# Nyström attention layer: scores in other PSUM banks, a variance one slot later, one block of attention in another place

## The chip, the cores and the metric

The kernel runs on one core of one Trainium2 chip. The time is device microseconds of one execution, the median of three. A profile is one execution of its own, with its own time.

## What is computed

The input x is (2, 512, 64, 32): two batches of 512 channels by 2048 tokens, all in fp32. Layer 0 is softmax attention with eight heads of 64 channels, frequency and time embeddings appended to the channels of its queries and keys, and a residual. Layer 1 normalises its input, and applies Nyström attention with 256 landmarks, a residual convolution of 33 tokens over the values, an output projection with bias, and a residual. A feed-forward map with a norm follows, again with a residual. Cut to layer 1 and the map, the computation is:

```
q, k, v = split(norm(x1) @ Wqkv)                      # 8 heads of 64, 2048 tokens
ql, kl  = mean of q, k over groups of 8 tokens         # 256 landmarks
attn1 = softmax(q kl^T / 8); attn2 = softmax(ql kl^T / 8); attn3 = softmax(ql k^T / 8)
z = pinv(attn2)                                        # 6 iterations of
    # z = 0.25 z (13 I - xz (15 I - xz (7 I - xz))),  xz = attn2 z
o = attn1 @ (z @ (attn3 @ v)) + conv33(v)
x2 = x1 + o @ Wout + bout
out = x2 + (normalised x2) @ map
```

## The kernel before, in words

**Engines and their order.** TensorE, VectorE, ScalarE and GpSimd take their instructions in the order in which the program writes them; no planner moves them. The DMAs are issued from SP's queue. So the order of the program's calls is the order of each queue, and an instruction that waits holds up all behind it on its engine.

**Tiles.** A block is 512 tokens (`TB`), so a batch has four blocks (`NTB`); channels lie in four chunks of 128 (`KC`). Heads go in pairs, four pairs (`NPAIR`) to a batch, eight in all. The kernel divides PSUM into eight banks of 128 x 512 fp32. In the stage that makes keys, queries and `attend` for batch 0's pairs, two of them are a ring `pp` that `bank(...)` hands out in turn, four are two double banks `sc` (`scores_bank`), two serve the values. In the later stage `pp` has four banks, a ring `pr` for the inverse's products has two (`product_bank`), and two side banks serve attn3's and attn1's values.

**Batch 0's pairs.** `attend` (L1243) makes attn2 of a pair: four products into `sc2` (L1254), exp (L1261), row sums and scaling on VectorE. It lies among the products of keys and queries (L1214), and among layer 0's last norm: its mean (L961) and variance (L974) with the sums of VectorE (L957, L958; squares L970, L971).

**The loop over pairs.** The main loop goes over `todo`: the four pairs of batch 1, then those of batch 0, n = 0 to 7. In turn n the pair in hand has its pseudo-inverse: five iterations of two squares, of `M` into `pa` and of `R` into `pb` (L1506), with VectorE updating `R` and `M` behind each (L1519). After each iteration `chunk(c)` puts in work of other pairs: block c of attn1 of the pair before (scores L1563, exp L1568, sum L1572, values L1579, row sums L1587, reciprocals L1595, ends L1600 and L1601) and the scores, exponentials, sums and values of attn3 of the pair after (L1335, L1344, L1349, L1356). Chunk 4 has landmarks and the convolution instead. Then come three products of another form (L1481), each with a flip (`tp`, L1490), and `last(0)` to `last(5)` stand between them; values of a later pair (L924) and other things are put in there.

**Finishing a block.** After turn 4 a generator `finish1_units` writes batch 1's outputs, block by block, in units that `advance(finish)` takes one at a time in the turns n = 5, 6 and 7, from `chunk`, from `last` and from a string of letters behind the loop. A block's units are: four output products `yp` with the residual added on VectorE (L939, L946); the sums and the mean (L957, L958, L961), the subtraction (L962), the squares on ScalarE and VectorE (L965 to L971), the variance (L974) and its root (L976), the reciprocal (L1625); and four products `fp` of the map (L1654) with y (L1646), the residual (L1647) and the store (L1648). A unit `GAP` takes one call without work. The residual `xb` is loaded (L1612) into a buffer that the next block uses too, tag `xr`, so that a load waits for the stores of the block before.

**The end.** Behind turn 7 a string gives the order of the last pair's attn1 (`1`), the finish units (`f`), batch 0's output products (`a`, `b`) and their norms (`s`, `t`). Then a loop over t does `map_units` for batch 0's four blocks, with the next block's norm between.

Of the kernel before, what the change touches and what calls it, by code (L numbers as in the profile page):

```python
# [16 lines left out]
P = 128  # L17
B, C, H, W = 2, 512, 64, 32
S = H * W
KC = C // P  # L20
# [641 lines left out]
def fast_path(  # L662
# [62 lines left out]
    def chunked(ap):  # L725
        return ap.rearrange("(k p) n -> p k n", p=P)

    def bank(name):
        return ps.tile([P, 512], F32, tag="pp", name=name)

    def scores_bank(name):
        return ps.tile([P, 2, 512], F32, tag="sc", name=name)
# [21 lines left out]
    def row_of(name):  # L754
        return apool.tile([P, TB], F32, tag="rinv", name=name)
# [37 lines left out]
    def gap(n=1):  # L793
        for _ in range(n):
            yield GAP
# [387 lines left out]
    class Pair:  # L1183
# [59 lines left out]
        def attend(self):  # L1243

            i, L = self.i, self.L
            X = self.X = [zpool.tile([P, 2, LM + 1], F32, tag=f"M{h}", name=f"X_{i}_{h}") for h in range(2)]
            rs = small.tile([P, 4], F32, tag="rs2", name=f"rs2_{i}")
            for h in range(2):
                nc.gpsimd.memset(X[h][:, :, LM:], 1.0)
            for h in range(2):  # L1250
                rows_h = slice(h * D, (h + 1) * D)
                sc = bank(f"sc2_{i}_{h}")
                for t in range(2):
                    nc.tensor.matmul(  # L1254
                        sc[:, t * LM : (t + 1) * LM],
                        lhsT=L[0][rows_h, t * P : (t + 1) * P],
                        rhs=L[1][rows_h, :],
                        start=True,
                        stop=True,
                    )  # L1260
                nc.scalar.activation(X[h][:, :, :LM], sc.rearrange("p (t n) -> p t n", n=LM), AF.Exp)  # L1261
            for h in range(2):
                two = slice(2 * h, 2 * h + 2)
                x_h = X[h][:, :, :LM]
                nc.vector.tensor_reduce(rs[:, two], x_h, AX.X, ALU.add)
                nc.vector.reciprocal(rs[:, two], rs[:, two])
                nc.vector.tensor_tensor(
                    x_h, x_h, rs[:, two].unsqueeze(2).to_broadcast([P, 2, LM]), ALU.mult
                )
                nc.sync.dma_start(X_d[self.b, self.hp, h], x_h)  # L1270
                nc.vector.tensor_reduce(rsum[:, i, two], x_h, AX.X, ALU.add)
# [54 lines left out]
            self.av3 = side_bank(3, f"av3_{self.name}")  # L1326
            self.p3 = {}

        def attn3_scores(self, s):
            scs = [bank(f"sc3_{self.name}_{s}_{h}") for h in range(2)]  # L1330
            for j in range(2):
                for h in range(2):
                    rows = slice(h * D, (h + 1) * D)
                    c = 2 * s + j
                    nc.tensor.matmul(  # L1335
                        scs[h][:, j * LM : (j + 1) * LM],
                        lhsT=self.k[rows, c * P : (c + 1) * P],
                        rhs=self.L[0][rows, :],
                        start=True,
                        stop=True,  # L1340
                    )
            p = self.p3[s] = exps(f"p3_{self.name}_{s}")
            for h in range(2):
                nc.scalar.activation(p[:, h, :], scs[h], AF.Exp)  # L1344
# [258 lines left out]
    class Finish1:  # L1603
# [25 lines left out]
        def norm_units(self):  # L1629
            steps = self.steps(lambda: deviation(self.name))  # L1630
            next(steps)
            yield GAP
            next(steps)
            yield
            next(steps)
            yield GAP
            next(steps)
            yield

        def map_units(self, bank_of):  # L1640


            def rest(m, fp):
                xb, toks = self.xb, slice(self.t * TB, (self.t + 1) * TB)
                y = row_of(f"y_{self.name}_{m}")
                nc.vector.tensor_tensor(y, fp, self.rstd, ALU.mult)  # L1646
                nc.vector.tensor_tensor(xb[:, m, :], y, xb[:, m, :], ALU.add)  # L1647
                nc.sync.dma_start(chunked(out[self.b])[:, m, toks], xb[:, m, :])  # L1648

            last = None  # L1650
            for m in range(KC):
                fp = bank_of(m, f"fp_{self.name}_{m}")
                for k in range(KC):
                    nc.tensor.matmul(  # L1654
                        fp, lhsT=mT[:, k, m * P : (m + 1) * P], rhs=self.xn[:, k, :],
                        start=k == 0, stop=k == KC - 1,
                    )
                if last is not None:
                    rest(*last)
                last = m, fp  # L1660
                yield
            rest(*last)

# [204 lines left out]
    for n, pair in enumerate(todo):  # L1868
        before = todo[n - 1] if n else None
        after = todo[n + 1] if n + 1 < len(todo) else None  # L1870
        if n + 2 < len(todo):
            todo[n + 2].prefetch_w()
        if n == NPAIR + 2:
            before.load_o(kvpool.tile([P, S], F32, tag="k", name=f"o2_{n - 1}"))
        if n == NPAIR + 3:
            before.load_o(late_buffer(f"o2_{n - 1}"))
        pair.iteration_start()
        while vals:
            advance(vals)
        if after:  # L1880
            after.prefetch()
            after.attn3_begin()
        if n + 2 < len(todo):
            vals = [values(n + 2)]
        if n:
            q = late_buffer if n > NPAIR + 1 else lambda name: kvpool.tile([P, S], F32, tag="k", name=name)
            pair.prefetch1(q(f"q2_{pair.name}"))

        def chunk(c):
            nonlocal landmarks  # L1890
            if before and c:
                before.attn1_inverse(c - 1, 1)
                before.attn1_end(c - 1)
            advance(finish)
            if c == NTB:
                if after:
                    landmarks = after.landmarks_values()
                    next(landmarks)
                    drain(convolution(n + 1))
                else:  # L1900
                    advance(finish, 2)
                return
            if before:
                if c:
                    before.attn1_scores(c, 0)
                    before.attn1_scores(c, 1)
                before.attn1_add(c)
            if after:
                for s in (2 * c, 2 * c + 1):
                    after.attn3_scores(s)  # L1910
                    after.attn3_add(s)
            else:
                advance(finish)
            if before:
                before.attn1_values(c)
            if after:
                after.attn3_values(2 * c)
            else:
                advance(finish)
            if before:  # L1920
                before.attn1_sums(c)
            if after:
                after.attn3_values(2 * c + 1)
            if before:
                before.attn1_inverse(c, 0)
            if n == NPAIR + 2 and c % 2:
                advance(finish)

        def last(i):
            nonlocal start  # L1930
            if i == 1 and after:
                next(landmarks)
                drain(landmarks)
                start = after.start_values()
            if i == 2 and after:
                next(start)
            else:
                advance(vals)
            if i == 3 and after:
                next(start)  # L1940
            if i == 5:
                pair.attn1_scores(0, 0)
                pair.attn1_scores(0, 1)
            advance(finish)

        landmarks = start = None
        pair.pinv(chunk, last)
        if n == NPAIR:
            finish.append(finish1_units(1, [p.o for p in todo[:NPAIR]]))
# [43 lines left out]
    st = [f.steps(deviation_of(t)) for t, f in enumerate(fs)]  # L1993

    ones_last = last_attn1()
    for c in "1f1f1f1f1f1fa1a1a1a1s1bs1s1b1bbt":
        if c == "f":
            advance(finish)
        else:
            next({"1": ones_last, "a": outs[0], "b": outs[1], "s": st[0], "t": st[1]}[c])  # L2000
# [13 lines left out]
    nc.gpsimd.partition_all_reduce(bad, oks, P, bass_isa.ReduceOp.max)  # L2014

    for t in range(NTB):
        maps = fs[t].map_units(wide_banks)
        if t + 1 < NTB:
            if t:
                next(st[t + 1])  # L2020
            turns(maps, None, st[t + 1], None, st[t + 1], None, None, st[t + 1])
        else:
            drain(maps)
        if t + 2 < NTB:
            drain(outs[t + 2])
# [89 lines left out]
```

## Time and profile before

| what | us |
|---|---|
| median of three runs | 2808.86 (2808.78 to 2810.7) |
| the profiled execution | 2808.29 |
| its span, first to last instruction | 2806.2 |
| TensorE busy | 2745.0 (98%) |
| VectorE busy | 1778.3 (63%) |
| ScalarE busy | 913.5 (33%) |
| GpSimd busy | 231.7 (8%) |

The mean granted clock of TensorE was 0.993. A line of the timeline has the start and the duration in microseconds, the engine, the line of the program, the operation, the tile written and the tiles read, the shape, the number of instructions run together, and in brackets the idle time before with the engine, tile and line that ended it. A line of waits has who waited, for whom, the microseconds in total, how often, and the longest. Products in fp32 appear as two rows each, so that eight products count as sixteen.

### The profile page before, as it was taken

What the parts mean: (1) busy time and instruction counts of PE and PEld (TensorE: products, weight loads), DVE (VectorE), ACT (ScalarE), POOL (GpSimd) and SP (SyncE); (2) the same over time, 40 slices, a digit from 0 to 9 for tenths busy, and PEclk for the clock granted to TensorE, in tenths of its full rate; (3) what the DMA queues carried; (4) which work ended last, traced back from release to release, by engine and by line L of the source; (5) the groups of instructions that cost most, each with busy time, mean ns of one, the idle gap of its engine ahead of it and who ended that gap; (6) DMA issues with size and microseconds to landing.
All of it is one profiled execution on the core that took longest, in us unless ns stands there. A gap on an engine that the chain in (4) does not pass through costs nothing. (4 is left out here: it accounts for less than half of the span.)

```text
span 2806.2 us, 39647 instructions
## 1 busy us (share of the span) xinstructions
PE 2745.0 (98%) x16746; PEld 1374.3 (49%) x16746; DVE 1778.3 (63%) x2109; ACT 913.5 (33%) x1352; POOL 231.7 (8%) x130
## 2 busy tenths in 40 slices
PE   9999999999999999999999999999999999999899
PEld 5343443434343334343344455777667666554333
DVE  2868788784658775767767544545755655556565
ACT  1434343433334334434422223223332323222110
POOL 1101101010101210100002000000100100000000
PEclk9999999999999999999999999999999999999999
DMA  3000000101001200002025632203001102010201
GB/s 113 5 5 1 5 1 1 61 16 46 27 32 60 75 1 1 1 31 67 16 83 180 202 120 89 97 28 114 27 28 50 65 1 86 23 61 19 101 16 46
DMA packets 85626, 140.31 MB, mean 50 GB/s; under 512 B 7856, under 2 KB 42944, under 8 KB 82880
## 3 DMA queue, kind: packets, MB, share of 16 engines
q1 hardware_dynamic: 80944, 120.87, 12.8%
q0 software_dynamic: 4416, 16.79, 1.6%
q8 instruction: 133, 2.18, 0.3%
q14 instruction: 53, 0.43, 0.0%
q10 hardware_dynamic: 80, 0.03, 0.0%
HBM read 82.48 MB, written 55.19 MB: 49 GB/s over the span
## 5 line engine op out<-in xcount | busy, mean ns | idle before, releaser
L1058 DVE TENSOR_TENSOR acc_f<-acc_f,p_f 128x1024 f32<-128x1024 f32 x448 | 611.4, 1365 | 217.8 <-ACT p_f L1048 188.8
L1048 ACT ACTIVATE p_f<-sc_f 128x1024 f32<-128x1024 f32 x512 | 496.8, 1022 | 580.2 <-PE sc_f L1040 574.1
L1040 PE MATMUL sc_f<-q_f,k_f 64*64 64x512 f32 x4096 | 491.7, 595 | 2.9 <-ACT p_f L1048 2.9
L1070 PE MATMUL av_f<-p_f,v_f 64*64 64x512 f32 x4096 | 484.3, 589 | 0.0
L1070 PEld LDWEIGHTS av_f<-p_f,v_f 64*64 64x64 f32 x4096 | 156.5, 133 | 283.0 <-issue 283.0
L1040 PEld LDWEIGHTS sc_f<-q_f,k_f 64*64 64x64 f32 x4096 | 144.8, 133 | 293.8 <-issue 253.0
L1214 PE MATMUL pp<-xh,w 128*128 128x512 f32 x512 | 231.2, 604 | 4.6 <-ACT X L1261 3.9
L1214 PEld LDWEIGHTS pp<-xh,w 128*128 128x128 f32 x512 | 95.7, 192 | 125.8 <-issue 113.9
L1506 PE MATMUL pb<-R 128*128 128x192 f32 (+1 forms) x640 | 149.6, 380 | 1.0 <-DVE M L1519 1.0
L1506 PE MATMUL pa<-M 128*128 128x192 f32 (+1 forms) x640 | 150.6, 380 | 0.0
L1595 DVE RECIPROCAL acc<-acc 128x256 f32<-128x256 f32 x64 | 111.4, 1746 | 46.7 <-ACT acc L1590 46.7
L1089 POOL TENSOR_TENSOR q_f<-q_f,rinv_f 128x512 f32<-128x512 f32 x32 | 68.3, 2135 | 825.6 <-DVE rinv_f L1088 825.5
L1601 POOL TENSOR_TENSOR o<-o,acc 128x512 f32<-128x512 f32 x32 | 53.8, 1682 | 885.1 <-DVE acc L1600 778.1
L924 PE MATMUL vp<-w,xh 128*128 128x128 f32 x1024 | 122.3, 278 | 0.0
L924 PEld LDWEIGHTS vp<-w,xh 128*128 128x128 f32 x1024 | 118.6, 194 | 7.2 <-issue 4.2
L924 PEld LDWEIGHTS vp_f<-wv_f,x 128*128 128x128 f32 x1024 | 115.6, 192 | 12.7 <-issue 11.0
L879 PE MATMUL pp_q_f<-x,wq_f 128*128 128x512 f32 x256 | 117.5, 612 | 4.2 <-DVE q_f L882 3.1
L939 PE MATMUL yp_f<-q_f,wo_f 128*128 128x512 f32 x256 | 115.9, 606 | 4.2 <-DVE rinv_f L1088 3.3
L924 PE MATMUL vp_f<-wv_f,x 128*128 128x128 f32 x1024 | 118.5, 276 | 0.0
L1506 PEld LDWEIGHTS pb<-R 128*128 128x128 f32 x640 | 106.5, 190 | 24.4 <-DVE M L1519 2.1
L1506 PEld LDWEIGHTS pa<-M 128*128 128x128 f32 x640 | 108.2, 193 | 20.4 <-ACT M L1497 2.5
L1654 PE MATMUL fp_g<-xn_g,mT 128*128 128x512 f32 x256 | 115.1, 598 | 0.7 <-ACT p L1568 0.7
(202 smaller groups left out, 3009.6 us busy)
## 6 DMA issues: line engine op xcount, KB each, us to landing
xh<-xh_fd SPq DMA_DIRECT2D x12, 1024.0 KB, 5.4
xr_f<-in_x_dram SPq DMA_DIRECT2D x8, 1024.0 KB, 5.1
x_fd<-xr_f POOLq DMA_DIRECT2D x8, 1024.0 KB, 4.7
xh_fd<-xn_f POOLq DMA_DIRECT2D x8, 1024.0 KB, 4.6
k_fd<-k SPq DMA_DIRECT2D x32, 256.0 KB, 2.7
q_fd<-q SPq DMA_DIRECT2D x32, 256.0 KB, 3.0
xb_g<-x_fd SPq DMA_DIRECT2D x32, 256.0 KB, 4.5
k<-k_fd SPq DMA_DIRECT2D x8, 1024.0 KB, 5.9
```

What stands on the lines that cost most here:

```text
L879: nc.tensor.matmul(pp, lhsT=w_sb[kind][:, k, cols], rhs=xbs[t][:, k, :], start=k == 0, stop=k == KC - 1)
L924: nc.tensor.matmul(vp[:, j * P : (j + 1) * P], lhsT=xb[:, k, j * P : (j + 1) * P], rhs=w_of(k), start=k == 0, stop=k == KC - 1,)
L939: nc.tensor.matmul(yp, lhsT=wo_sb[:, k, m * P : (m + 1) * P], rhs=oTs[k][:, toks], start=k == 0, stop=k == NPAIR - 1,)
L1040: nc.tensor.matmul(sc[r * D : (r + 1) * D, h, :], lhsT=hd.k[rows, lo : lo + D], rhs=hd.q[rows, t * TB : (t + 1) * TB], start=True, stop=True,)
L1048: nc.scalar.activation(p, sc, AF.Exp, scale=D**-0.5)
L1058: nc.vector.tensor_tensor(acc, first if c == 1 else acc, p, ALU.add)
L1070: nc.tensor.matmul(av[r][half, :], lhsT=hd.v[keys, c, half], rhs=pp[keys, h, :], start=c == 0, stop=c == NST - 1,)
L1089: nc.gpsimd.tensor_tensor(o, o, rinv, ALU.mult)
L1214: nc.tensor.matmul(pp, lhsT=self.w[j][:, c, :], rhs=xhs[t][:, c, :], start=c == 0, stop=c == KC - 1)
L1506: nc.tensor.matmul(dst, lhsT=lhsT[:, k, t * P : (t + 1) * P], rhs=rhs[:, k, :], start=k == 0, stop=k == 1)
L1595: nc.vector.reciprocal(half, half)
L1654: nc.tensor.matmul(fp, lhsT=mT[:, k, m * P : (m + 1) * P], rhs=self.xn[:, k, :], start=k == 0, stop=k == KC - 1,)
```

## The change

It has five parts. For pairs 0 to 2 of batch 0 `attend` takes both heads' scores from one double bank `sc` in place of two banks of `pp`. In each chunk the first of attn3's two score blocks takes the two product banks `pr` in place of two of `pp`. In the finishing units the variance comes two free calls behind its squares in place of one, and so each later unit of batch 1 moves by one call for each block done. In turns 6 and 7 the fourth block of attn1 of the pair before is taken out of chunk 3, and stands in `last(0)` to `last(5)`. The very last product of the map is made in two halves of 256 columns, each with its own y, residual and store. The string of the last turns is changed to hold the two more units that are left over.

```diff
         def attend(self):
+            scs = scores_bank(f"sc2_{i}") if i + 1 < NPAIR else None
...
-                sc = bank(f"sc2_{i}_{h}")
+                sc = scs[:, h, :] if scs is not None else bank(f"sc2_{i}_{h}")
...
-        def attn3_scores(self, s):
-            scs = [bank(f"sc3_{self.name}_{s}_{h}") for h in range(2)]
+        def attn3_scores(self, s, bank_of=bank):
+            scs = [bank_of(f"sc3_{self.name}_{s}_{h}") for h in range(2)]
...
         def norm_units(self):
...
             next(steps)
-            yield GAP
+            yield from gap(2)
             next(steps)
             yield
...
-        def map_units(self, bank_of):
+        def map_units(self, bank_of, parts=1):
-            def rest(m, fp):
-                xb, toks = self.xb, slice(self.t * TB, (self.t + 1) * TB)
-                y = row_of(f"y_{self.name}_{m}")
-                nc.vector.tensor_tensor(y, fp, self.rstd, ALU.mult)
-                nc.vector.tensor_tensor(xb[:, m, :], y, xb[:, m, :], ALU.add)
-                nc.sync.dma_start(chunked(out[self.b])[:, m, toks], xb[:, m, :])
+            def rest(m, fp, cols):
+                xb, toks = self.xb, slice(self.t * TB + cols.start, self.t * TB + cols.stop)
+                y = row_of(f"y_{self.name}_{m}_{cols.start}")[:, cols]
+                nc.vector.tensor_tensor(y, fp[:, cols], self.rstd[:, cols], ALU.mult)
+                nc.vector.tensor_tensor(xb[:, m, cols], y, xb[:, m, cols], ALU.add)
+                nc.sync.dma_start(chunked(out[self.b])[:, m, toks], xb[:, m, cols])
...
+                n = TB // (parts if m == KC - 1 else 1)
+                for lo in range(0, TB, n):
+                    cols = slice(lo, lo + n)
+                    for k in range(KC):
+                        nc.tensor.matmul(
+                            fp[:, cols], lhsT=mT[:, k, m * P : (m + 1) * P], rhs=self.xn[:, k, cols],
+                            start=k == 0, stop=k == KC - 1,
+                        )
+                    if last is not None:
+                        rest(*last)
+                    last = m, fp, cols
...
         def chunk(c):
-            if before and c:
+            if before and 0 < c <= n_ones:
                 before.attn1_inverse(c - 1, 1)
                 before.attn1_end(c - 1)
...
-            if before:
+            ones_before = before if c < n_ones else None
+            if ones_before:
...
-                for s in (2 * c, 2 * c + 1):
-                    after.attn3_scores(s)
+                for s, bank_of in ((2 * c, product_bank), (2 * c + 1, bank)):
+                    after.attn3_scores(s, bank_of)
                     after.attn3_add(s)
...
         def last(i):
+            if n_ones < NTB:
+                if i == 0:
+                    before.attn1_scores(n_ones, 0)
+                    before.attn1_scores(n_ones, 1)
+                    before.attn1_add(n_ones)
+                if i == 1:
+                    before.attn1_values(n_ones)
+                if i == 2:
+                    before.attn1_sums(n_ones)
+                if i in (3, 4):
+                    before.attn1_inverse(n_ones, i - 3)
+                if i == 5:
+                    before.attn1_end(n_ones)
...
+        n_ones = NTB if n + 2 < len(todo) else NTB - 1
         pair.pinv(chunk, last)
...
-    for c in "1f1f1f1f1f1fa1a1a1a1s1bs1s1b1bbt":
+    for c in "f1f1f1f1f1f1f1fa1a1a1as11bs1bs1bbt":
...
-        maps = fs[t].map_units(wide_banks)
+        maps = fs[t].map_units(wide_banks, 1 if t + 1 < NTB else 2)
```

## The prediction

> **What bounds the kernel now.** I read the page's busy line first, then TensorE's waits, then TensorE's timeline around each long one, and last VectorE's waits. The busy line (busy us, share of the span, instructions):
>
> ```profile
> span 2806.2 us, 39647 instructions
> PE 2745.0 (98%) x16746; PEld 1374.3 (49%) x16746; DVE 1778.3 (63%) x2109; ACT 913.5 (33%) x1352; POOL 231.7 (8%) x130
> ```
>
> TensorE is the bound. The change removes none of its work, so it can win only from the 61 us that it idles (2806.2 − 2745.0) and from matmuls that run slower than their like. Its waits (for whom: total, times, longest):
>
> ```profile
> PE var_g L974 <- DVE sq_g L971: 12.3, 4, 4.4
> PE mean_g L961 <- DVE xn_g L958: 5.9, 3, 3.0
> PE pp L1214 <- ACT X L1261: 3.9, 2, 2.7
> PE rs L1587 <- DVE acc L1572: 2.4, 3, 1.8
> ```
>
> The first is the variance that is moved, the third the `attend` that gets other banks. The timeline (start, duration, idle before) shows what a wait costs beside its own length:
>
> ```profile
> 1521.72 1.92 PE L1254 MATMUL sc<-L,L 64*128 64x256 f32 x8
> 1526.32 6.78 PE L1214 MATMUL pp<-xh,w 128*128 128x512 f32 x8 [2.68 <-ACT X L1261]
> 1532.93 1.02 PE L974 MATMUL var_n<-xr_f,mean_w 128*128 128x512 f32 x2
> ...
> 1883.54 2.58 PE L1335 MATMUL sc<-L,k 64*128 64x256 f32 x16
> ...
> 2360.99 1.10 PE L974 MATMUL var_g<-sq_g,mean_w 128*128 128x512 f32 x2 [2.49 <-DVE sq_g L971]
> ...
> 2567.89 2.04 PE L974 MATMUL var_g<-sq_g,mean_w 128*128 128x512 f32 x2 [4.40 <-DVE sq_g L971]
> ```
>
> Eight L1214 matmuls take 3.68 us at 1510.02 but 6.78 behind the 2.68 us gap, and a variance 2.04 instead of 1.10 behind the 4.40 us gap: the granted clock was halved. Sixteen score matmuls (L1335) take 2.58 us in a chunk; where their banks are free, 1.93. VectorE, in its timeline and its waits:
>
> ```profile
> 1529.38 0.69 DVE L971 TENSOR_TENSOR xr_f<-xr_f 128x512 f32<-128x512 f32 x1
> ...
> 1784.75 0.75 DVE L1519 SCALAR_TENSOR_TENSOR M<-M,pb 128x320 f32<-128x320 f32 x2 [1.09 <-PE pb L1506]
> ...
> 2422.34 0.75 DVE L946 SCALAR_TENSOR_TENSOR xb_g<-yp_g,b_f,xb_g 128x512 f32<-128x512 f32 x1 [6.07 <-DMA xb_g<-x_fd]
> ```
>
> ```profile
> DVE xb_g L946 <- DMA xb_g<-x_fd: 18.4, 3, 6.2
> ```
>
> VectorE has slack on average, but three times it stands some 6 us on a load that must wait for a store, with everything behind it.
>
> **What the Trainium skill says.** "TensorE: Matmul & The Clock Gate", "What's actually happening": after an idle window the clock falls to half, and the window of 3413 ns runs freely. The trace agrees: half-clock stretches are 3.41 or 6.83 us long; gaps of 2.49, 2.68, 3.03 and 4.40 us, and the pair 2.36 + 2.41, have one; 1.81, 2.05 and one of 3.01 have none. So one costs 1.7 or 3.4 us, and whether a gap gets it is partly luck. "PSUM — Partial Sum Buffer", "PSUM bank collisions raise a hardware error": two engines must not touch a bank at once; so a product waits for the last reader of its bank, as `pp` waits for ScalarE's `X`. "Perfetto Trace Analysis", "Sequencer Loop": an instruction waits in its engine's queue for its semaphores; the 6.07 us stall above holds up VectorE's queue just so.
>
> **The change part by part** (gain positive, against the profiled execution).
>
> *A, attend in a double bank (pairs 0 to 2 of batch 0).* Its eight matmuls take 1.92 to 2.04 us because the two heads' banks are the ring of the products round them; the same eight take 1.07 to 1.14 in the later stage, with no such wait: 0.85 each. Pair 0: 0.7, since the mean behind it can't start before VectorE's sum ends at 1464.82 (it started 1465.24). Pair 1: at stake are the gap 2.68, the half clock 3.3 (6.78 less 3.5) and 0.85 = 6.8; but the next thing in TensorE's queue that matters, var_n, needs VectorE's L971, which ends at 1530.07 and whose predecessors do not get earlier. TensorE then waits there about 3.75 us, with a half clock again: I take 1.0. Pair 2: 1.23 + 0.85 = 2.1. Sum 3.8; 9.6 if var_n isn't late, −1 if its half clock is long.
>
> *B, first block of attn3's scores in product banks.* In chunks 1 to 3 with n = 1 to 5 the 2.58 becomes 1.93: 0.65, of which I count 0.58 × 15 = 8.7 (mean of the chunks 2.51). But where the scores follow pinv's last square directly (n = 0, four chunks; chunk 0 of n = 1 to 4), head 1's product bank is still read by VectorE: L1519 at 1784.75 ends at 1785.50, TensorE comes at 1784.64. 4 × 0.45 (in n = 0 the exponentials bind anyway) + 4 × 0.94 = 5.6 lost. Net 3.1; 8.7 if the wait costs nothing, −11 if VectorE is as late in the other fifteen chunks (15 × (0.58 − 0.94) − 5.6).
>
> *C, variance one slot later, n = 5's end.* The gap at 2360.99 (2.49) and half clock (five groups 5.22 instead of 3.67, 1.55 + some) go; tp's wait of about 1.15 for ScalarE's copy of R, behind the squares, comes: 3.4 with the 0.5 that the variance itself ran long.
>
> *D, n = 6, with the fourth attn1 block in the last products.* Chunk 0: 0.9 (scores 2.87 to 1.93). Chunk 1: 3.0: the gap 1.81 at `rs` and the stalled scores of 1.2, both since VectorE stood 6.07 us at L946 behind the load. Every finish step is one call later, so that same L946 now stands right ahead of R in chunk 2: TensorE's next square waits for R, about 4.0, and 0.7 × 1.7 half clock: −5.2. Queued behind it on VectorE are R, M and the sums, and for R waits TensorE. Chunk 2 +0.6 by its scores, chunk 3 nothing, chunk 4 +1.1 (part sums no longer ahead of R: gap 0.60, and 0.5). Last products +3.0: gaps 0.46 + 3.03 and a half clock 1.7 go, 2.0 for R behind the mean's subtraction comes; 0.2 is taken off for the block's own waits. The block moved (20 matmul rows, four exponentials, a sum, two reciprocals, two ends, no DMA) costs as much there as in chunk 3. Sum 3.4.
>
> *E, n = 7 to the last blocks (2513 to 2667).* Before, gaps and half clocks sum to 24.8: 2.55 near 2551, 4.40 + a half clock of 3.4 at 2567.89, 1.55 in two small gaps, 8.15 in five gaps up to 2637.46 (among them 2.36 and 2.41), 3.4 for the half clock with them, 1.3 in three. After, by the same queues: 1.3 (first xb load ahead of pinv's R), 6 (the mean waiting for its part sums about 3.75, then ScalarE's squares ahead of the flips), 2.5 (a product behind the third load and ScalarE's 1.28 us table load), 1.9 in small ones, 5.9 where `rs` stands behind the square sums, 3.4 for two half clocks behind the two long ones: 21.0. Gain 3.8; this is my least certain term, −6 to 11.
>
> *F, the string of the last turns.* The mean's gap of 3.01 at 2694.74 and 0.38 + 0.45 go, as both its sums stand two units ahead: 3.8.
>
> *G, last product in halves.* After TensorE's end the y and xb (0.69 each) and a 256 KB store remain. At half width 0.35 each: 0.7, and a little of the store, less 0.2 for eight shorter matmuls: 0.8. VectorE's first half is hidden by the second half's products; the extra DMA stands alone on SP's queue.
>
> Sum: 3.8 + 3.1 + 3.4 + 3.4 + 3.8 + 3.8 + 0.8 = 22.1. The profiled execution took 2808.3 us, 0.6 below the median shown, and so 2808.3 − 22.1 = 2786.2: I forecast 2786 us.
>
> **The rivals.**
> *R1, the waits only move.* Each gap of C, D and E comes back at its new place with a half clock, as in A pair 1. For: VectorE's order is the only thing changed there. Against: the variance's new slots have 2 to 4 us of products between. Then C, D, E give about 0 and A 1: 1 + 3.1 + 3.8 + 0.8 = 8.7, 2800 us.
> *R2, none of the new stalls comes.* A 9.6, B 8.7, C 3.4, D 8.6, E 11.4 (without `rs` and its half clock), F and G 4.6 = 46.3: 2762. For: my stalls are inferred from start times that shift by a few us. Against: the xb load's 6 us is measured three times.
> *R3, slower: VectorE stands on xb's load right ahead of pinv's R at the three block borders.* Forecast there 4.0 + 1.3 + 2.75 = 8, from stalls of 6.06. From 15 us each (9 longer, 27 in all, less the gain of 22.1) the change loses 5: 2813, and more beyond. Against: the longest of the three waits is 6.2.
> *R4, product banks late in all chunks.* B at −11 takes 14.1 from the sum: 2800; with R1's zero for C to E, 11 more, 2811. For: the wait at 1784.64 is there in each chunk of n = 0. Against: in the fifteen, attn1's scores (1.99 at 1881.72) stand between the square and attn3's scores.
>
> **How the numbers follow.** Forecast, a gain of 11 to 34: 0.64. R2, more than 34: 0.11. R1: 0.12, three quarters of it a gain over 0.2%. R3: 0.06. R4: 0.07, of which 0.04 faster, 0.03 the same. A measurement of this kernel can tell 0.2%, 5.6 us, from no change. Faster 0.64 + 0.11 + 0.09 + 0.04 = 0.88; same 0.03 + 0.03 = 0.06; slower 0.06. The range runs from 2774 (halfway to R2) to 2803 (past R1), leaving out R3, half of R4 and most of R2; the forecast's own range is 2776 to 2797.
>
> **What would show it.** A: L1254 at about 1.1, no `pp` wait for `X`, but a var_n wait near 3.75 in pair 1. B: the sixteen L1335 at 1.93 in chunks 1 to 3, a new wait of `sc` for M (L1519) in n = 0. C and D: var_g for sq_g much below 12.3, a wait of `pa` or `pb` for R behind L946. E: a wait of `rs` (L1587) near 5.9. F: no mean gap near 2680. G: the last y and xb at 0.35. I am wrong if VectorE's stalls at the loads land where TensorE has work, or are followed by several half clocks more than the five of before.

## The result, and the profile after

The changed kernel takes 2798.06 us (median of six runs, 2796.39 to 2799.18) against 2808.82 before, ratio 0.9962 with a 95% interval of 0.9950 to 0.9975. It is faster, and the time lies in the range, but the gain is 10.8 us where 22.8 were forecast: less than half. Measured again beside later experiments it has a ratio of 0.9957 (0.9941 to 0.9974). The page of the kernel after:

```profile
span 2795.8 us, 39629 instructions
PE 2736.7 (98%) x16754; PEld 1374.5 (49%) x16754; DVE 1776.0 (64%) x2111; ACT 913.5 (33%) x1352; POOL 231.6 (8%) x130
```

TensorE is busy for 8.3 us less, though it has the same work in a few more rows. Attn3's scores have 6.8 us of that (76.7 us in all before, 69.9 after): their rows no longer hold the wait for a bank. The half clock has no part in it, since its stretches between 1500 and 2700 us sum to 27.3 us in both traces. TensorE's idle time is 59.1 us in place of 61.2, so hardly any of the waits' sum is gone. The waits of TensorE after show why:

```profile
PE sc L1255 <- ACT X L1262: 6.2, 3, 3.5
PE rs L1588 <- DVE acc L1573: 5.4, 1, 5.4
PE mean_g L961 <- DVE xn_g L958: 4.2, 1, 4.2
...
PE p_pb L1497 <- DVE R L1520: 2.7, 1, 2.7
PE wp L1482 <- DVE R L1520: 2.6, 2, 1.7
PE sc L1336 <- DVE M L1520: 1.7, 8, 0.2
...
PE wp L1482 <- ACT o L1446: 1.3, 1, 1.3
```

The variance's 12.3 us are gone from the list, and so are the 3.9 of `pp` for `X`. In their place stand two waits that no line of the prediction has, of `attend`'s scores for `X` and of `wp` for ScalarE's `o` at the end of n = 5, and, as forecast, waits of `rs`, of the mean, of `p_pb` for R and of attn3's scores for M.

To give each stage its share I took the start of the same group of instructions in both traces, and took off the work that one of the two had done by then and the other not (a product of four `yp` or `fp` rows at 3.43 us, and so on, from the trace of before). What the lead changes by between two such points is the stage's gain, in us:

| part | forecast | measured |
|---|---|---|
| A, attend | +3.8 | −3.3 |
| B, banks of attn3's scores | +3.1 | +3.4 |
| C, end of n = 5 | +3.4 | +3.2 |
| D, n = 6 | +3.4 | +1.5 |
| E, n = 7 | +3.8 | +2.1 |
| F, last turns | +3.8 | +3.5 |
| G, last product | +0.8 | 0.0 |
| sum | 22.1 | 10.4 |

The sum is that of the two spans, 2806.2 − 2795.8; the single parts hold to about half a microsecond, since the borders and the price of the work enter. Of the 11.7 us that are missing, A has 7.1, D 1.9, E 1.7 and G 0.8. Pair 1's `attend` in TensorE's timeline after (start, duration, idle before and what ended it):

```profile
1522.53 1.13 PE L1255 MATMUL sc<-L,L 64*128 64x256 f32 x4
1527.14 1.13 PE L1255 MATMUL sc<-L,L 64*128 64x256 f32 x4 [3.48 <-ACT X L1262]
1528.19 5.36 PE L1214 MATMUL pp<-xh,w 128*128 128x512 f32 x8
1533.39 1.02 PE L974 MATMUL var_n<-xr_f,mean_w 128*128 128x512 f32 x2
```

and ScalarE's at the same place:

```profile
1524.12 1.05 ACT L968 ACTIVATE xr_f<-xn_f 128x1024 f32<-128x1024 f32 x1
1525.19 1.28 ACT L1262 ACT_TABLE_LOAD   x1
1526.48 0.60 ACT L1262 ACTIVATE X<-sc 128x512 f32<-128x512 f32 x1
```

The eight rows of scores are now split in two fours. Head 1's start at 1527.14, just behind the end of head 0's exponential (1526.48 + 0.60): TensorE no longer waits behind the scores, for a bank of `pp`, but between them, until ScalarE has done the squares, a table load and the exponential. The gap is longer too (3.48 against 2.68), and `pp` still takes 5.36 us in place of 3.7 at half clock. Chunk 2 of n = 6, VectorE and then TensorE:

```profile
2424.65 0.75 DVE L946 SCALAR_TENSOR_TENSOR xb_g<-yp_g,b_f,xb_g 128x512 f32<-128x512 f32 x1 [6.02 <-DMA xb_g<-x_fd]
2425.32 0.74 DVE L1520 SCALAR_TENSOR_TENSOR R<-M,pa 128x320 f32<-128x320 f32 x2
```

```profile
2425.85 0.48 PE L1497 MATMUL p_pb<-ident,R 128*128 128x128 f32 x1 [2.74 <-DVE R L1520]
2426.78 1.65 PE L1507 MATMUL pb<-R 128*128 128x192 f32 x4 [0.45 <-DVE M L1520]
```

This is the forecast's new stall, where it was said to be: L946 behind the load, R behind L946, TensorE behind R. The four `pb` rows take 1.65 us instead of 0.82, at half clock.

The last instructions of VectorE after:

```profile
2785.99 0.69 DVE L1647 TENSOR_TENSOR y_g<-fp_g,rstd_g 128x512 f32<-128x512 f32 x1 [2.02 <-PE fp_g L1658]
...
2789.44 0.42 DVE L1647 TENSOR_TENSOR y_g<-fp_g,rstd_g 128x256 f32<-128x256 f32 x1 [2.04 <-PE fp_g L1658]
2789.90 0.42 DVE L1648 TENSOR_TENSOR xb_g<-y_g,xb_g 128x256 f32<-128x256 f32 x1
2790.24 0.42 DVE L1647 TENSOR_TENSOR y_g<-fp_g,rstd_g 128x256 f32<-128x256 f32 x1
2790.70 0.43 DVE L1648 TENSOR_TENSOR xb_g<-y_g,xb_g 128x256 f32<-128x256 f32 x1
```

and of the kernel before:

```profile
2796.52 0.69 DVE L1646 TENSOR_TENSOR y_g<-fp_g,rstd_g 128x512 f32<-128x512 f32 x1 [2.02 <-PE fp_g L1654]
...
2799.95 0.69 DVE L1646 TENSOR_TENSOR y_g<-fp_g,rstd_g 128x512 f32<-128x512 f32 x1 [2.02 <-PE fp_g L1654]
2800.68 0.69 DVE L1647 TENSOR_TENSOR xb_g<-y_g,xb_g 128x512 f32<-128x512 f32 x1
```

The first half's y starts 3.45 us behind the y of the product before, which is the length of the whole product (before: 2799.95 − 2796.52 = 3.43). Both halves' operations stand behind TensorE's end, 1.69 us in place of before's 1.42; from the y at 2785.99 to the end of the span are 9.8 us, and from the y at 2796.52 before 9.7, so nothing is won.

### The profile page after: what moved, and what is told of

The parts are those of the page before. It is cut to its first block, busy times and chain, and to the rows that moved or that the text cites. A ratio compares the mean times of both kernels' runs of the same rounds, so it can differ in the third digit from the quotient of the medians.

```text
span 2795.8 us, 39629 instructions
## 1 busy us (share of the span) xinstructions
PE 2736.7 (98%) x16754; PEld 1374.5 (49%) x16754; DVE 1776.0 (64%) x2111; ACT 913.5 (33%) x1352; POOL 231.6 (8%) x130
## 4 chain that ended last, share of the span: by engine, by line
PE 87%; DVE 9%; ACT 1%; issue 1%; DMA 1%; POOL 0%; DVEq 0%; SPq 0%; ACTq 0%; POOLq 0%
PE sc_f L1040 13%; PE av_f L1070 13%; PE pp L1214 8%; PE pb L1507 5%; PE pa L1507 5%; PE vp_f L924 4%; PE vp L924 4%; PE pp_k_f L879 4%; PE fp_g L1658 4%; DVE acc_f L1058 4%; PE yp_g L939 3%; PE yp_f L939 3%; PE pp_q_f L879 3%; PE sc L1564 2%; PE sc L1336 2%; PE av L1357 2%
## 5 line engine op out<-in xcount | busy, mean ns | idle before, releaser
L939 PE MATMUL yp_g<-o,wo_f 128*128 128x512 f32 x256 | 115.5, 598 | 0.8 <-ACT p L1569 0.8
```

Source lines behind the costliest of these rows:

```text
L939: nc.tensor.matmul(yp, lhsT=wo_sb[:, k, m * P : (m + 1) * P], rhs=oTs[k][:, toks], start=k == 0, stop=k == NPAIR - 1,)
```

## The experiments

My theory for A and G was one: the kernel waits for a tile, not for the part of it that is read. Where two heads or two halves lie in one tile, the second's products wait for the reader of the first (A), or the reader of the first for the products of the second (G). The rival for A was ScalarE's order. For D and E the theory was that VectorE's stand at the load of `xb` costs what the later variance wins, with the moved block covering further waits; the rivals were that the later variance or the moved block lose in themselves.

### Attend as before, in the changed kernel

```diff
-            scs = scores_bank(f"sc2_{i}") if i + 1 < NPAIR else None
+            scs = None
```

> The changed kernel with attend's scores back in two pp banks, all else as changed. Theory 1 (in one tile head 1's products wait for the exponential of head 0; three such waits, 6.2 us in all, and the half clocks behind them make the stage 3.5 us longer than before): 2794.5 us, the three waits of sc for X are gone, the waits of pp for X (3.9 us) are back. Rival (the stage's loss has another cause, such as the queue of ScalarE in another order): 2798 us, and the stage from the first sc of pair 0 to the first pr of pair 2 stays 3.5 us longer than before.

2792.86 us, ratio 0.9947 (0.9930 to 0.9963). From the first scores of pair 0 to the first `pr` of pair 2 the stage is 0.1 us from the length that it has before. The wait of `pp` for `X` is back at 3.9 us, and that of `sc` gone. The time agrees with the first theory; its interval overlaps the changed kernel's, so the stage's length is the firmer proof.

### Each head in a tile of its own

```diff
-                sc = scs[:, h, :] if scs is not None else bank(f"sc2_{i}_{h}")
+                sc = scores_bank(f"sc2_{i}_{h}")[:, 0, :] if i + 1 < NPAIR else bank(f"sc2_{i}_{h}")
```

> The changed kernel with each head's scores of attend in a double bank of its own (the first half of it), in the same order of instructions. Theory 1 (the wait is for the tile, not for the bank or ScalarE): the three waits of sc for X vanish, eight products take 1.1 us, pair 1 waits at the variance for about 3.7 us, and the time is 7.3 below the changed kernel: 2790.8 us. Rival a (the wait vanishes but the variance and its half clock take all of it in pair 1): 2794 us. Rival b (ScalarE's exponential is waited for whatever the tile): 2798 us.

2788.29 us, ratio 0.9932 (0.9915 to 0.9948). No wait of `sc` for `X` is left. TensorE's timeline of this kernel, pair 1:

```profile
1520.41 1.14 PE L1254 MATMUL sc<-L,L 64*128 64x256 f32 x8
1521.48 3.70 PE L1214 MATMUL pp<-xh,w 128*128 128x512 f32 x8
1528.87 2.05 PE L974 MATMUL var_n<-xr_f,mean_w 128*128 128x512 f32 x2 [3.69 <-issue]
```

The eight scores take 1.14 us in one run, `pp` follows at once, and TensorE stands 3.69 us at the variance with a half clock after it: to the letter what the prediction had put at this place for the double bank (3.75, an estimate from VectorE's L971). The order of the instructions is the same and only the tile differs, so the wait is for the tile. The stage gains 2.6 us on the kernel before, where 3.8 was forecast: the half clock here is a long one of 6.8 us. (At n = 6 this trace has no half clock at all, which is no gain of the edit.)

### The double bank in attend alone

The edit is the change's first part, put into the kernel before.

> The kernel before with the double bank in attend alone. Theory (the wait of head 1 for head 0's exponential in the same tile): three waits of sc for X of 6.2 us, the stage from the first sc of pair 0 to the first pr of pair 2 some 3.5 us longer, 2811 us. Rival (the double bank costs only beside the other edits): 2804 to 2808 us.

2812.02 us, ratio 1.0016 (1.0009 to 1.0023): slower. Its waits have the same new line:

```profile
PE var_g L974 <- DVE sq_g L971: 11.5, 4, 4.4
PE sc L1255 <- ACT X L1262: 6.2, 3, 3.5
```

The stage is 4.3 us longer than before (a lag of 1.5 at its start grows to 5.9). Part A loses by itself. In each of the seven traces that have the double bank beside other parts of the change, the stage is 3.3 to 3.4 us longer than before.

### The second half of the last product in another bank

```diff
-                fp = bank_of(m, f"fp_{self.name}_{m}")
...
                     cols = slice(lo, lo + n)
+                    fp = bank_of(m - 1 if lo else m, f"fp_{self.name}_{m}_{lo}")
```

> The changed kernel with the second half of the last product in a bank of its own. Theory 1 (in the changed kernel the first half's y waits for the whole product, 2789.44 being the end of both halves, so that the four half operations stand behind one another for 1.7 us): y of the first half starts some 1.7 us earlier, behind TensorE's end stand 0.9 us of VectorE in place of 1.7, and the end comes 0.8 earlier in the profile. Rival (the wait is on TensorE's count and not on the tile): the same as the changed kernel.

```profile
2787.29 0.69 DVE L1647 TENSOR_TENSOR y_g<-fp_g,rstd_g 128x512 f32<-128x512 f32 x1 [2.02 <-PE fp_g L1658]
...
2789.02 0.42 DVE L1647 TENSOR_TENSOR y_g<-fp_g,rstd_g 128x256 f32<-128x256 f32 x1 [0.31 <-PE fp_g L1658]
...
2790.75 0.43 DVE L1647 TENSOR_TENSOR y_g<-fp_g,rstd_g 128x256 f32<-128x256 f32 x1 [0.84 <-PE fp_g L1658]
2791.21 0.42 DVE L1648 TENSOR_TENSOR xb_g<-y_g,xb_g 128x256 f32<-128x256 f32 x1
```

The first half's y comes 1.73 us behind the full-width y before it, and is done while TensorE makes the second half. From that full-width y to the end of the span (2796.1) are 8.8 us; in the changed kernel 2795.8 − 2785.99 = 9.8, before 2806.2 − 2796.52 = 9.7. So in the traces the part is worth its 0.8 once the halves have a bank each. The edit gives the second half another tile and another bank at once; which of the two the wait was for stays open. The whole time, 2797.87 us of one run, can't show 0.8.

### The variance one slot behind its squares, in the changed kernel

```diff
-            yield from gap(2)
+            yield GAP
...
-    for c in "f1f1f1f1f1f1f1fa1a1a1as11bs1bs1bbt":
+    for c in "1f1f1f1f1f1fa1a1a1a1s1bs1s1b1bbt":
```

> The changed kernel with the variance one slot behind its squares as before, and the string of the last turns of before; banks, the moved block and the halves as changed. Theory 1 (the later slot is worth 3.2 at n = 5, 3.5 in chunks 0 and 1 of n = 6, 2.1 at n = 7 and 3.5 in the string, and costs 7.0 where R waits behind the load of xb in chunk 2 of n = 6): 2798 + 12.3 - 7.0 = 2803 us, and the wait of p_pb for R (2.7 us) is gone. Rival (the later slot costs more than it wins, since each block's loads and sums are put in front of R, the mean and rs): 2790 us, with the mean's 4.2 and rs's 5.4 us gone too.

2802.45 us, ratio 0.9982 (0.9972 to 0.9992), as the first theory had it. The wait of `p_pb` for R is gone from its trace, and the variance's waits are back at 10.9 us in four. By the medians the later slot is worth some 5 us net, and the interval just touches the changed kernel's (0.9950 to 0.9975); it is no mistake, though it creates waits of its own.

### The load of the residual earlier

```diff
+        xb = block_of(lpool, "xr", f"xb_g_{b}")
         for t in range(NTB):
-            xb = block_of(lpool, "xr", f"xb_g_{b}_{t}")
...
+        def load_next(self, m):
+            for k in range(max(m - 1, 0), m + m // (KC - 1)):
+                self.load(self.t + 1, k)
...
                 nc.sync.dma_start(chunked(out[self.b])[:, m, toks], xb[:, m, cols])
+                behind(m)
```

`load` is the load of one quarter as before, and `behind` is `load_next` for batch 1's first three blocks.

> The changed kernel with one xb tile for batch 1's four blocks, each quarter of the next block's residual loaded one product after the store of the same quarter, so that L946 does not stand on store plus load. Theory 1 (that stall holds up R in chunk 2 of n = 6, with 7.0 us lost, and parts of the waits at n = 7): VectorE's three waits of xb_g for its load (18.1 us) go to under 3, the waits of p_pb for R (2.7) and pb for M go, and the time is 7 to 11 below the changed kernel: 2789 us. Rival (TensorE then waits somewhere else for the same VectorE work): 2796 us or more.

2788.56 us, ratio 0.9934 (0.9918 to 0.9951). VectorE's wait of `xb_g` for its load, 18.1 us in the changed kernel, is no longer in the list. TensorE in chunk 2 of n = 6:

```profile
2419.84 1.89 PE L1507 MATMUL pa<-M 128*128 128x192 f32 x8
2421.57 0.27 PE L1497 MATMUL p_pb<-ident,R 128*128 128x128 f32 x1
2421.68 1.89 PE L1507 MATMUL pb<-R 128*128 128x192 f32 x8
```

The square follows without a gap and at full clock. From the first `pa` of this iteration to that of the next are 19.1 us here and 25.8 in the changed kernel's trace (2419.38 to 2445.18), so the stall cost 6.7 there, where the forecast had 5.2. From the first `pa` of n = 6 to the last `wp` of n = 7 this kernel wins 8.8 us on that trace.

### Product banks only where other products stand ahead

```diff
-                for s, bank_of in ((2 * c, product_bank), (2 * c + 1, bank)):
+                for s, bank_of in ((2 * c, product_bank if before and (c or n > NPAIR) else bank), (2 * c + 1, bank)):
```

> The changed kernel with attn3's first score block in the product banks only where other products stand between it and the last square (chunks 1 to 3 from n = 1, and all of n = 5 and 6), in pp elsewhere. Theory 1 (by stages of the trace the eight direct ones lose 4 x 0.5 + 4 x 0.9 us, the others win 0.7 each): 5.6 below the changed kernel, 2792.4 us, and the eight waits of sc for M are gone. Rival (the loss in the eight is by ScalarE, which is not changed by the bank): 2798 us.

2793.59 us, ratio 0.9952 (0.9935 to 0.9968): of the sign expected, but within the intervals not to be told from the changed kernel. The trace tells it: the eight waits of `sc` for M are gone, and over the eight places the lead on the changed kernel grows by 5.65 us (0.32 to 5.97). The prediction's 5.6 for this loss was right.

### The moved block back in chunk 3, and the moved block alone

```diff
-        n_ones = NTB if n + 2 < len(todo) else NTB - 1
+        n_ones = NTB
```

> The changed kernel with attn1's fourth block back in chunk 3 at n = 6 and 7; the variance, banks and halves as changed. Theory 1 (the block covers the waits between the last products: about 3 us at n = 6, little at n = 7): 2801 us. Rival (the block in the last products brings the wait of rs for its sum, 5.4 us and a half clock, at n = 7): 2793 us, and that wait is gone.

2791.56 us, ratio 0.9938 (0.9921 to 0.9954): below the changed kernel's time with an interval that overlaps, and not above it as my theory had it; but the rival's reason does not hold either, since its wait of `rs` stays at 5.3 us. In the trace, taking the block back loses 0.4 us from the first `pa` of n = 6 to that of n = 7, with a half clock of 3.4 us that the changed kernel's trace lacks, and wins 3.0 at n = 7. TensorE at n = 7 in the changed kernel, and then in this one:

```profile
2598.56 1.98 PE L1564 MATMUL sc<-q,L 64*128 64x512 f32 x6
2601.00 1.12 PE L1564 MATMUL sc<-q,L 64*128 64x512 f32 x2 [0.46 <-ACT p L1569]
...
2612.45 1.27 PE L1482 MATMUL wp<-M,R 128*64 128x256 f32 x8 [0.98 <-DVE R L1520]
```

```profile
2608.01 3.60 PE L939 MATMUL yp_g<-o,wo_f 128*128 128x512 f32 x8
2611.54 1.14 PE L1482 MATMUL wp<-M,R 128*64 128x256 f32 x8
```

With the block there its scores wait for ScalarE's exponentials, and the product waits for R; without it neither gap is there. To see whether the block is bad in itself, I put the block alone into the kernel before:

> The kernel before with attn1's fourth block of n = 6 and 7 in the last products alone. Theory (block and later variance cover the same waits between the last products, so that the second of them only costs): alone the block wins, its 4 us of products filling the 3.03 us gap with its half clock at n = 6 and part of the 6.5 us of gaps at n = 7: 2802 us. Rival (the block costs about 3 us there by itself, since its exponentials, sum and reciprocals stand ahead of R): 2811 us.

2801.10 us, ratio 0.9976 (0.9965 to 0.9986): alone it wins. At n = 6 the variance's gap of 3.03 us shrinks to 2.35, at n = 7 the product's gap of 0.82 for R goes. Part of the profile's gain (2.2 us at the point where the edits begin) has nothing to do with the edit; between there and the start of the last blocks it gains 5.0 us, and in the last turns it gives 2.4 back, in a half clock of 6.8 us behind the same 3.01 us gap of the mean that has none in the trace of before. So the block wins alone and, beside the later variance, costs 3.0 us at n = 7: the two seem to work on the same gaps. The later variance still wins beside the block (the kernel with the variance one slot behind is the slower), and it was not run alone. The cost of the block in the changed kernel (ratios 0.9938 and 0.9962 or 0.9957, with overlapping intervals) rests on one trace of each.

### The mended parts together

> The changed kernel with the edits of the four kernels with own tiles in attend, early loads, chosen banks and the tail's bank together. If their gains add: 2798 - 7.3 - 9 - 5.6 - 0.8 = 2775 us. If the early loads only move the wait: 2783 us.

2775.04 us, ratio 0.9889 (0.9872 to 0.9905): the gains add. With the block back in chunk 3 as well:

> The kernel with own tiles in attend, early loads, chosen banks and the tail's bank, and with attn1's fourth block back in chunk 3. If the block in the last products costs 3 us there too: 2772 us. If it only covered waits that the early loads have taken away: the same 2775 us.

2773.83 us, ratio 0.9879 (0.9862 to 0.9895). This beats both kernels, by 34 us and, against the changed kernel's time measured beside it, by 22. From the kernel without this last edit the times do not tell it; in the traces it is 1.6 us shorter (spans 2771.1 and 2772.7), less than the 3 that I had put. Beside these last kernels the changed kernel was run again:

> The changed kernel itself, on the same chip as the others of this call: 0.9962 of the time before, 2797 us.

2795.47 us, ratio 0.9957. Its four times lie in two pairs, 2793.5 and 2793.7, 2797.3 and 2797.4. The profiled one is of the first pair, with a span of 2791.9 us against 2795.8 in the trace above; its start is 1.9 us faster before any edit comes, and two of its half clocks, at n = 6 and n = 7, are 3.4 us long in place of 6.8. The square behind the stall at n = 6:

```profile
2423.73 0.33 PE L1497 MATMUL p_pb<-ident,R 128*128 128x128 f32 x1 [2.71 <-DVE R L1520]
2424.66 3.44 PE L1507 MATMUL pb<-R 128*128 128x192 f32 x8 [0.60 <-DVE M L1520]
2427.94 0.27 PE L1497 MATMUL p_pb<-ident,R 128*128 128x128 f32 x1
2428.05 1.89 PE L1507 MATMUL pb<-R 128*128 128x192 f32 x8
```

The second eight rows are at full clock again. D gains 1.5 us more in this trace than in the first, 3.0 of its 3.4, while A loses the same 3.4.

## Why the prediction was wrong

The direction was right and so was the reading of what bounds the kernel. The size was wrong, mostly by one step, A.

**A failed in its mechanism.** The step said that with a double bank the eight matmuls lose the wait for the ring round them, "0.85 each". They do lose it; but the step took the two heads in one tile to be as free of each other as two tiles. They are not: head 1's products wait for head 0's exponential, 6.2 us in three waits. In the kernel before the heads had a tile each, so its trace could not show this. A gained nothing of its 3.8 and lost 3.3, which is 7.1 of the 11.7 us missing. The trace of the double bank with a tile for each head shows all that A had said: 1.14 us, and 3.69 at the variance where 3.75 was put. The range of A (−1 to 9.6) did not hold the −3.3, because its lower end was taken from the half clock alone.

**G failed by a like step**, for 0.8: "VectorE's first half is hidden by the second half's products" holds only if the first half may be read while the second is written. Both halves lie in one bank, and the prediction itself had read that two engines must not touch a bank at once, so its own rule spoke against G. With a bank each it is hidden, and the 0.8 is there.

**D's price was right, and its half clock fell badly.** The stall behind the load of `xb` was put at 4.0 us and 0.7 of a short half clock, 5.2. Against the 19.1 us of the iteration without the stall, it took 6.7 more in the first trace of the changed kernel, with a long half clock behind it; 5.3 in the second, with a short one; and 3.9 with a tile for each head, where none came. So 1.5 of the 1.9 us that D misses belong to one execution and not to the forecast.

**E failed by a term put at nothing.** The moved block was counted as a gain at n = 6's end and at nothing for n = 7, while the variance's later slot was credited with gaps there; with the block in its old chunk the trace is 3.0 us shorter at n = 7. The waits forecast for E came at their sizes: the mean 4.2 (3.75 put) and `rs` 5.4 (5.9 put).

**B, C and F were right** in mechanism and nearly in size: the win in the fifteen chunks was 0.7 each (0.58 put), the loss in the eight direct ones 5.65 (5.6 put), the mean's gap of 3.01 is gone. B's chunks make 4.7 together; about 1 us of it was lost again in the wait of `wp` for ScalarE's `o` (1.3 us, after 0.3 at this place before), which leaves the table's 3.4.

Of the rivals, R1, waits that only move, gave 2800 and is nearest in time, but it is not what happened: C and F gained as forecast, and what fell away was in A, which R1 had at +1. R3's stall was real, but its price stayed near the 6 us of the loads. The Trainium skill's "TensorE: Matmul & The Clock Gate", "What's actually happening", was used for the half clock, and these runs agree with its length: all stretches but the last of a run are 3.4 us or a multiple. They differ from its table in what brings one: it has an idle window of about 3.4 us, and here gaps of 2.5 us were followed by one. Its "PSUM — Partial Sum Buffer", "PSUM bank collisions raise a hardware error", was read as if the bank were all that is kept apart. It speaks of two engines at one bank; the wait in A was between the two banks of one tile, so no collision of banks asks for it. In G both halves share a bank.

## What to carry to other kernels

Two things that are to proceed independently should have a tile each, even if they lie in different banks: in A a slice of a shared tile waited for the reader of the other slice. When two edits aim at the same gap, count it once, and price the second by what it puts in front of the next wait. Move a load ahead of the point where its reader stands in front of the critical engine, rather than only shuffle the work round it: with the tile for each head, that gave the largest single gains found here, some 7 to 8 us each by the medians.

## What was not expected of the hardware

The same gap can be followed by no half clock, by one of 3.4 us or by one of 6.8. Behind the 2.68 us gap of pair 1 the eight `pp` took 6.78 us before, and 5.16 in the changed kernel with attend as before. Behind the mean's 3.01 us gap in the last turns there was none before, and 6.8 us with the moved block alone. In two executions with the earlier variance the gaps near 2630 us were followed by 10.2 us.

The traces show what decides. In each trace the half clocks start a whole number of windows of 3.413 us apart, so they lie on a fixed grid. Of the 100 that start after the first 30 us and before the end, in the 14 traces, 98 start behind a window of the grid in which TensorE was idle for 2.0 us or more. The other two follow windows of 1.2 and 1.3 us in which eight score rows took 1.92 us in place of 1.1, so that a wait is hidden in the busy time. None of the 10 900 other windows at full clock had more than 1.94 us. The mean's gap before is cut by the grid into 1.35 and 1.66 us; with the moved block alone 2.6 us of it lie in one window. The stall at n = 6 left 2.74 and 2.71 us in one window in the two traces of the changed kernel, and at most 1.94 in that of a tile for each head, which has no half clock there. A stretch went on for another window whenever its last one had at least 0.45 us idle, and ended whenever it had less than 0.36; in the two traces of the changed kernel it was 0.453 us at n = 6, and went on, and 0.445, and ended.

So a gap is worth more than its length only if it fills enough of one window, and a shift of a few tenths of a microsecond against the grid can change that. With TensorE busy all through it, a window at half clock costs 1.7 us (an estimate, half of its length). Stages with the same instructions then differ by that much and more, so a gain of 2 us or less in a stage is read from its gaps, or from several traces, and not from one length.
